# A graph network's second layer: block 11 moves from the count matrices to the gathers

## The chip, the cores and the metric

The kernel runs on one core of a Trainium2 chip. The metric is the device time of one execution in microseconds. Comparisons use the median of several executions; profiles show one execution.

## The reference

6250 nodes with 256 features, 100,000 edges sorted by destination, and a loop at each node. Three graph convolutions, widths 512, 512 and 256, then a residual sum and a layer norm:

```python
deg = jax.ops.segment_sum(jnp.ones_like(dst, dtype=x.dtype), dst, num_segments=n)   # with the loops
dinv = jnp.where(deg > 0, jax.lax.rsqrt(deg), 0.0)
norm_edge = dinv[src] * dinv[dst]
h = x
for W, b in ((W1, b1), (W2, b2), (W3, b3)):
    # h @ W, each edge's source row scaled by norm_edge, summed over its destination, + b
    h = jax.nn.relu(_gcn_layer(h, W, b, src, dst, norm_edge, n))
x = _layernorm(x + h, axis=-1)
```

Since sum and matrix product commute, the kernel sums the scaled rows first and multiplies by W afterwards, where that is cheaper.

## The kernel before

**Blocks and chunks.** The nodes lie in 50 blocks of 125. A block's incoming edges lie in 16 chunks of 128 (`KF`), and what goes beyond them in a chunk that ten blocks share. Each layer sums the neighbours of a block in one of two ways:

- *Gathered*: for each chunk POOL issues an indirect DMA that fetches 128 rows of the layer's table (L1186; in layer 2 a row has 512 floats, 2 KB; in layer 3 it has 256). In layers 2 and 3 ACT casts the landed row to the first part of a two-part number (L1240), DVE takes the rest (L1243), and TensorE multiplies both parts by a one-hot matrix of the destinations, which DVE makes by comparison (L1136), and adds the products in PSUM (L1213: two matmuls of 512 columns for a chunk in layer 2).
- *By count matrices*: in layer 1 the kernel counts, for some blocks, how many edges lead from each node to each node of the block, and keeps these counts as bytes in DRAM (`kept`, 6250 x 125 for a block). A block's sum is then the product of its counts with all 50 blocks of rows.

**Layer 2.** Blocks 0 to 11 are summed by count matrices, in three groups of four (`TEAM`, `TEAMS`), and blocks 12 to 49 are gathered (38 x 16 chunks and a shared one at the first block and at each ten). The generator `teams` does the groups, one after the other. For each of the 50 source blocks (a unit) it loads the rows (two units a load), casts and splits them (L934, L936), casts the counts of the group's blocks from bytes (L926, one cast for each block and five units), and multiplies (L979): four banks, one for each quarter of the 512 features, two matmuls each, with the group's blocks beside each other in the columns, 4 x 125 = 500. After the 50th unit DVE scales each bank by the destinations' `dinv` (L914) and the group's two couples of blocks go through W2 and W3 (`hidden`).

**Order.** There is no scheduler on the chip; the order on each engine is written out by a loop over the chunks in `layer` (L1230). In each step it issues the gather of its chunk, the cast of the chunk three before, the subtraction of the chunk four before, the products of the chunk nine before (six at the end of the layer), and then lets the generators that are due run to their next `yield`, which says after how many chunks they are due again. `teams` yields one chunk for each bank, 23 times in 24 (`PACE`), so that a unit takes about four chunks, whatever its columns are:

```python
if in_layer == 0 and pairs_done % 3 or in_layer == 1 and (pairs_done % PACE if now >= EAGER else pairs_done % 3 == 0):
    yield 1
```

Landed rows of layer 2 go round seven buffers, and their two parts round eight, with three more that are lent as long as the groups run.

**After a block.** `after2` transposes the sum of a gathered block (L1294) and waits for a second one; every two blocks in a row go through W2 and W3 together, and the last two (`ALONE`) alone. `hidden` has one PSUM bank for all (`take("win", 1)`): the products with W2 (L1366, 250 columns for a couple, 125 for one block, eight matmuls in a step), ReLU on ACT (L1372), the products with W3 (L1379), scaling (L1390), and a store to layer 3's table. It waits up to `TO_PE` = 5 chunks between its steps, only one chunk in the last 32 chunks of a layer. The result is also kept in SBUF (`parts`) for layer 3, unless the place is taken by the groups' buffers, which lie over blocks 17 and up (`HOME`); such blocks are read back from the table by `home` once the groups have ended.

**Layer 3** gathers blocks 29 to 49 and sums the others by their count matrices (L1273). Some of its products are made ahead while layer 2's last steps run (L1036). Its first gather waits for the last store of layer 2.

Of the kernel before, what the change touches and what calls it, by code (L numbers as in the profile page):

```python
# [22 lines left out]
P = 128  # L23
# [3 lines left out]
Q = 125  # L27
# [28 lines left out]
EXTRAS_AFTER = (3, 6, 9, 11, 13, 15, 17)  # L56
TEAM = 4
TEAMS = 3
HOME = 17
MANY = 29  # L60
ALONE = 2
# [335 lines left out]
def sorted_path(ctx: ExitStack, tc: tile.TileContext, x, edges, starts, found, wts, biases, room, late, out):  # L397
# [492 lines left out]
    def teams(groups):  # L890

        nonlocal teams_done, returning
        units = [(g, k) for g in range(len(groups)) for k in range(NB)]

        def fetch_counts(g, c):
            for n, b in enumerate(groups[g]):
                by_rows(nc.sync, team_used[(g * CUTS + c) // 2 % 2][n].rearrange("p k v -> p (k v)"), kept[b][:, c * PIECE * Q:(c + 2) * PIECE * Q])

        def next_counts(g, c):
            if c + 2 < CUTS:  # L900
                fetch_counts(g, c + 2)
            elif g + 1 < len(groups):
                fetch_counts(g + 1, c + 2 - CUTS)

        def load(p):
            if 2 * p < len(units):
                k = units[2 * p][1]
                by_rows(nc.sync, streamed[p % RING], tables[1][k * Q:(k + 2) * Q, :].rearrange("(b p) c -> p b c", p=Q))

        def load_scales(g):  # L910
            nc.sync.dma_start(out=scales, in_=dinvs[g * TEAM:(g + 1) * TEAM, :].rearrange("b p -> (b p)").unsqueeze(0).to_broadcast([P, TEAM * Q]))

        def scaled(g, n):
            nc.vector.tensor_tensor(team_zt[:, n], team_banks[n][:, :TEAM * Q], scales, op=ALU.mult)  # L914
            free(f"team{n}")
            if n == TEAM - 1:
                if g + 1 < len(groups):
                    load_scales(g + 1)
                yield SOON
                team_ended[0](hidden(groups[g][:2], team_zt[:, :, :2 * Q], "tz"))  # L920
                for _ in range(4 * KF if g + 1 < len(groups) else 2 * KF):
                    yield 1
                team_ended[0](hidden(groups[g][2:], team_zt[:, :, 2 * Q:], "tz"))

        def piece(g, c, n):
            nc.scalar.copy(team_pieces[(g * CUTS + c) % 2][:, :, n * Q:(n + 1) * Q], team_used[(g * CUTS + c) // 2 % 2][n][:, c % 2 * PIECE:(c % 2 + 1) * PIECE, :])  # L926
            if c % 2 and n == TEAM - 1:
                next_counts(g, c - 1 + 2)

        def half(u, h):  # L930
            if u < len(units):
                to, row = both_parts[u % 3], streamed[u // 2 % RING][:, u % 2, :]
                if h == 0:
                    nc.scalar.copy(to[:, :HID], row)  # L934
                else:
                    nc.vector.tensor_sub(to[:, HID:], row, to[:, :HID].bitcast(F32))  # L936

        while products < FEW * NB - KF:
            yield 1
        fetch_counts(0, 0)  # L940
        for p in range(RING):
            load(p)
        fetch_counts(0, 2)
        yield 6
        load_scales(0)
        while finished < FEW:
            yield 1
        for bank in team_banks:
            while not any(b is bank for b in common):
                yield 1  # L950
            del common[next(n for n, b in enumerate(common) if b is bank)]
        half(0, 0)
        for n in range(TEAM):
            piece(0, 0, n)
            if n % 2:
                yield 1
        half(0, 1)
        half(1, 0)
        yield 1
        half(1, 1)  # L960
        pairs_done = 0
        for u, (g, k) in enumerate(units):
            if u == len(units) - RETURN:
                returning = now
            if u % 2:
                load((u + 1) // 2 + RING - 1)
            for n in range(TEAM):
                if k == 0:
                    yield from take(f"team{n}", 1)
                if k == NB - 1 and n == 0:  # L970
                    while held.get("tz", 0):
                        yield 1
                    held["tz"] = TEAM // 2
                if 1 <= n < 3:
                    half(u + 2, n - 1)
                if k % PIECE == 2 and u + PIECE < len(units):
                    piece(*divmod(g * CUTS + k // PIECE + 1, CUTS), n)
                for h in range(2):
                    nc.tensor.matmul(team_banks[n][:, :TEAM * Q], lhsT=both_parts[u % 3][:, h * HID + n * P:h * HID + (n + 1) * P],  # L979
                                     rhs=team_pieces[(g * CUTS + k // PIECE) % 2][:, k % PIECE, :],  # L980
                                     start=(k == h == 0), stop=(k == NB - 1 and h == 1))
                if k == NB - 1:
                    team_ended[0](scaled(g, n))
                pairs_done += 1
                if in_layer == 0 and pairs_done % 3 or in_layer == 1 and (pairs_done % PACE if now >= EAGER else pairs_done % 3 == 0):
                    yield 1
        teams_done = True
        assert not on_loan, (now, len(on_loan))
# [366 lines left out]
    def hidden(two, zt, name):  # L1355

        wide = len(two) * Q
        each = 4 // len(two)
        yield TO_PE
        yield from take("ht2", 1)  # L1360
        for f2 in range(0, KH, each):
            yield from take("win", 1)
            h_ps = win_bank[:, :4 * Q].rearrange("p (f v) -> p f v", f=each)
            for f in range(each):
                for k in range(KH):
                    nc.tensor.matmul(h_ps[:, f, :], lhsT=w2_sb[:, k, (f2 + f) * P:(f2 + f + 1) * P], rhs=zt[:, k, :],  # L1366
                                     start=(k == 0), stop=(k == KH - 1))
                yield 1
            if f2 + each == KH:
                free(name)  # L1370
            for f in range(each):
                nc.scalar.activation(ht2[:, f2 + f, :wide], h_ps[:, f, :], AF.Relu, bias=b2_sb[:, f2 + f:f2 + f + 1])  # L1372
            yield TO_PE
            free("win")
        yield from take("win", 1)
        u_ps = win_bank[:Q].rearrange("p (h c) -> p h c", h=2)
        for h in range(len(two)):
            for k in range(KH):
                nc.tensor.matmul(u_ps[:, h, :], lhsT=ht2[:, k, h * Q:(h + 1) * Q], rhs=w3_sb[:, k, :],  # L1379
                                 start=(k == 0), stop=(k == KH - 1))  # L1380
            yield 1
        free("ht2")
        u = work.tile([Q, HID], F32, name="st").rearrange("p (h c) -> p h c", h=2)
        if two[-1] == two[0] + 1:
            runs = [(slice(two[0], two[0] + 2), slice(0, 2))]
        else:
            runs = [(slice(p, p + 1), slice(h, h + 1)) for h, p in enumerate(two)]
        for to, h in runs:
            n = to.stop - to.start
            nc.vector.tensor_tensor(u[:, h], u_ps[:, h], dinv[:, to].unsqueeze(2).to_broadcast([Q, n, C]), op=ALU.mult)  # L1390
        for to, h in runs:
            by_rows(nc.sync, u[:, h], tables[2][to.start * Q:to.stop * Q, :].rearrange("(h p) c -> p h c", p=Q), store=True)
            if not teams_done and to.stop > HOME:
                waiting.extend(range(to.start, to.stop))
            else:
                nc.scalar.copy(parts[:, to, :C], u[:, h])
        here = [(to, h) for to, h in runs if to.start not in waiting]
        yield SOON
        for to, h in here:
            nc.vector.tensor_sub(parts[:, to, C:], u[:, h], parts[:, to, :C].bitcast(F32))  # L1400
        yield SOON
        free("win")
# [63 lines left out]
        if b in EXTRAS_AFTER:  # L1466
            made_in_order.append(FEW + EXTRAS_AFTER.index(b))
    assert sorted(made_in_order) == many
    groups = [every[g * TEAM:(g + 1) * TEAM] for g in range(TEAMS)]
    team_steps = teams(groups)  # L1470
    layer(0, C, every[FEW:], few, after1, first_rows, first, spacing, [(0, other_parts()), (2, both_stored(2 * GRP)), (0, searches), (1, counts(made_in_order, places)), (60, dinvs_stored()), (first, team_steps)], carried=team_steps)

# [2 lines left out]
    def last_weights():  # L1475
        load_w2()
        load_w3()
        yield 1
# [3 lines left out]
    split = split_rows_of(two, "swide_split", 1, HID)  # L1482
    split += loaned
    own_row = two.enter_context(tc.tile_pool(name="sown_row", bufs=1)).tile([P, HID], F32, name="own_row")[:Q]
    layer(1, HID, every[TEAM * TEAMS:], [], after2, wide_rows,
          extras=[(5, last_weights()), (0, team_steps), (20, home()), (steps(TEAM * TEAMS) - 2 * KF, fetch_first())], filler=ahead_of_time())
    assert begun % PIECE == 0
    there[:] = [0]
    fetch(many[1], 6)
# [188 lines left out]
```

## Time and profile before

| | |
|---|---|
| three executions | 2067.38, 2073.05, 2081.36 us (median 2073.05) |
| profiled execution | 2076.16 us; its span, from the first to the last instruction, 2074.4 us |
| mean granted TensorE clock | 0.961 |
| busy, share of the span | TensorE 93%, DVE 72%, POOL 68%, ACT 63% |
| DMA | 486.17 MB moved, mean 234 GB/s |

In the profile PE is the matmuls and PEld the weight loads that run under them; L979 is line 979 of the kernel. A row of a group gives engine, operation, tiles (out<-in), count, busy time, the mean of one in ns, and the idle time of the engine just before with what ended most of it. Ends of matmuls are modelled, so a sum of their durations can be more than the time they take; the distance between starts is the better measure. POOL's busy time is that of issuing a gather, not of the transfer.

### The profile page before, as it was taken

Reading aid. Unit: us, or ns where it says so; the run is one execution under the profiler, and the core shown is the slowest. Engines: PE = TensorE matmul, PEld = TensorE weight load, DVE = VectorE, ACT = ScalarE, POOL = GpSimd, SP = SyncE. Lnnn points to the kernel's source line nnn. Section 1 sums busy time; section 2 is a strip of 40 time slices with the busy share of each in tenths; the row PEclk is TensorE's granted clock in tenths of the full one; section 3 lists DMA queues with packets and bytes.
Section 4 is the critical chain, followed back from the end, with each engine's and each line's share of the span. In section 5 each row is a group of like instructions: output and inputs, shape, how many; then the busy total and the mean of one; then the engine's idle time right before and its main releaser. Section 6 shows DMA issues by size and latency. Waiting matters only on the chain. (4 is left out here: it accounts for less than half of the span.)

```text
span 2074.4 us, 30032 instructions
## 1 busy us (share of the span) xinstructions
PE 1923.9 (93%) x8642; PEld 1513.7 (73%) x8642; DVE 1494.1 (72%) x2809; ACT 1302.3 (63%) x2484; POOL 1418.2 (68%) x1442
## 2 busy tenths in 40 slices
PE   4399999999999688999999999999989899999996
PEld 3277777777776467778888878887767777777774
DVE  6877888888882376777766777677675467777776
ACT  2576777787884465766766656667565455556553
POOL 2467777766777377777776776677674577777775
PEclk6699999999999899999999999999999999999998
DMA  7898999999999999999999998978886466666674
GB/s 172 244 308 212 271 260 256 276 260 257 275 274 252 264 268 248 269 260 265 261 262 258 258 260 239 266 230 266 244 239 189 115 180 183 182 178 190 174 191 117
DMA packets 233624, 486.17 MB, mean 234 GB/s; under 512 B 44142, under 2 KB 87358, under 8 KB 233446
## 3 DMA queue, kind: packets, MB, share of 16 engines
q0 software_dynamic: 125184, 315.61, 54.6%
q1 hardware_dynamic: 94980, 159.23, 27.9%
q10 hardware_dynamic: 13282, 9.30, 1.7%
q8 instruction: 70, 1.15, 0.2%
q14 instruction: 108, 0.88, 0.1%
HBM read 416.51 MB, written 67.47 MB: 233 GB/s over the span
## 5 line engine op out<-in xcount | busy, mean ns | idle before, releaser
L1186 POOL DMA_INDIRECT room<-tab,ssrc x1008 | 1025.8, 1018 | 384.6 <-issue 162.6
L1243 DVE TENSOR_TENSOR halves<-room,halves 128x512 fp32r<-128x512 f32 (+1 forms) x806 | 453.4, 579 | 279.0 <-ACT halves L1240 273.0
L1240 ACT CAST halves<-room 128x512 fp32r<-128x512 f32 (+1 forms) x806 | 408.5, 528 | 286.0 <-DMA room<-tab,ssrc 244.7
L1213 PE MATMUL sacc<-halves,shot 128*125 128x512 f32 x1541 | 527.1, 406 | 38.8 <-DVE shot L1136 27.8
L1186 POOL DMA_INDIRECT halves<-both,ssrc x384 | 360.5, 939 | 143.3 <-issue 41.8
L1213 PEld LDWEIGHTS sacc<-halves,shot 128*125 128x125 f32 x1541 | 286.9, 188 | 120.4 <-ACT halves L1240 25.1
L785 DVE TENSOR_TENSOR room<-near_cols,slots 128x625 bf16<-128x625 f32 (+2 forms) x435 | 325.3, 804 | 30.8 <-PE sacc L852 12.7
L1145 ACT CAST piece<-room 125x625 fp32r<-125x625 uint8 x416 | 297.2, 722 | 70.4 <-PE win_ps L1273 19.2
L1136 DVE TENSOR_TENSOR shot<-near_cols,sdlo 128x500 fp32r<-128x500 f32 x371 | 248.0, 670 | 9.3 <-PE sacc L1213 4.8
L1366 PE MATMUL win_ps<-room,w_sb 128*128 128x250 f32 (+1 forms) x832 | 192.5, 375 | 1.6 <-ACT room L1372 1.6
L1273 PE MATMUL win_ps<-parts,piece 125*125 125x512 f32 x650 | 186.2, 405 | 6.2 <-ACT piece L1145 6.2
L1273 PE MATMUL smm<-parts,piece 125*125 125x512 f32 x655 | 188.9, 405 | 1.3 <-ACT piece L1145 0.7
L1366 PEld LDWEIGHTS win_ps<-room,w_sb 128*128 128x128 f32 x832 | 158.0, 195 | 25.3 <-ACT room L1372 2.0
L1273 PE MATMUL mat_ps<-parts,piece 125*125 125x512 f32 x600 | 172.4, 404 | 1.3 <-ACT piece L1145 1.3
L852 PEld LDWEIGHTS <-room 128*125 128x125 bf16 x725 | 95.8, 138 | 74.0 <-issue 23.0
L1273 PE MATMUL sacc<-parts,piece 125*125 125x512 f32 x450 | 147.6, 432 | 0.9 <-ACT piece L1145 0.9
L1273 PEld LDWEIGHTS win_ps<-parts,piece 125*125 125x125 f32 x650 | 119.3, 188 | 37.7 <-ACT piece L1145 8.0
L814 ACT CAST room<-sacc 125x500 uint8<-125x500 f32 (+1 forms) x155 | 107.6, 712 | 56.5 <-PE sacc L852 41.7
L1273 PEld LDWEIGHTS smm<-parts,piece 125*125 125x125 f32 x655 | 116.8, 187 | 29.3 <-issue 2.3
L936 DVE TENSOR_TENSOR parts<-parts 125x512 fp32r<-125x512 f32 x150 | 103.4, 689 | 41.6 <-ACT parts L934 41.6
L1273 PEld LDWEIGHTS mat_ps<-parts,piece 125*125 125x125 f32 x600 | 107.6, 186 | 29.4 <-ACT piece L1145 3.0
L1243 DVE TENSOR_TENSOR parts<-room,parts 128x512 fp32r<-128x512 f32 x138 | 93.4, 692 | 33.3 <-ACT parts L1240 32.9
(310 smaller groups left out, 2938.5 us busy)
## 6 DMA issues: line engine op xcount, KB each, us to landing
parts<-tab SPq DMA_DIRECT2D x81, 448.0 KB
kept<-room SPq DMA_DIRECT2D x29, 683.6 KB
room<-kept SPq DMA_DIRECT2D x29, 683.6 KB
tab<-st SPq DMA_DIRECT2D x74, 224.0 KB
room<-tab,ssrc POOLq DMA_INDIRECT x1008
both<-parts SPq DMA_DIRECT2D x10, 1120.0 KB
own_row<-tab SPq DMA_DIRECT2D x38, 224.0 KB
parts<-kept SPq DMA_DIRECT2D x60, 136.7 KB
```

Of the source, the lines that this page charges most:

```text
L785: nc.vector.tensor_tensor(out, near_cols[:, :shape[2]].unsqueeze(1).to_broadcast(shape), numbers.unsqueeze(2).to_broadcast(shape), op=ALU. ...
L814: nc.scalar.copy(place[:, :, u * G:(u + len(ms)) * G].rearrange("p k (t r) -> p t k r", r=G), counted_in[:Q, :len(ms) * 256].rearrange("p ...
L852: nc.tensor.matmul(bank[:Q, len(pair) * 256:][:, :G * NB], lhsT=hot_lo, rhs=hot_key, start=True, stop=True)
L936: nc.vector.tensor_sub(to[:, HID:], row, to[:, :HID].bitcast(F32))
L1136: nc.vector.tensor_tensor(hot[:, :n], near_cols[:, :Q].unsqueeze(1).to_broadcast([P, n, Q]), dlo.rearrange("p b j -> p (b j)")[:, at:at + ...
L1145: convert(piece, made_or_read[:, c * PIECE:(c + 1) * PIECE, :])
L1186: nc.gpsimd.indirect_dma_start(out=row, out_offset=None, in_=table, in_offset=bass.IndirectOffsetOnAxis(ap=at, axis=0))
L1213: nc.tensor.matmul(acc[:Q, :size], lhsT=hot, rhs=row[:, c0:c0 + size], start=(i == 1 and k == c0 == 0), stop=(k == KF and c0 + size == row ...
L1240: nc.scalar.copy(halves[:, :width], landed[chunk - hi_lag])
L1243: nc.vector.tensor_sub(halves[:, width:], landed.pop(chunk - lo_lag), halves[:, :width].bitcast(F32))
L1273: nc.tensor.matmul(acc_d[:Q], lhsT=got[done // PIECE][:, k % PIECE, :], rhs=parts[:, k], start=(k == 0), stop=(k == NB - 1))
L1366: nc.tensor.matmul(h_ps[:, f, :], lhsT=w2_sb[:, k, (f2 + f) * P:(f2 + f + 1) * P], rhs=zt[:, k, :], start=(k == 0), stop=(k == KH - 1))
```

## The change

The third group has three blocks, 8 to 10, instead of four. Its matmuls read 376 columns instead of 500 (three blocks are 375, made even), the casts and loads of counts of a fourth block are left out, and `hidden` gets block 10 alone as the group's second part. Block 11 is gathered: the layer's list begins with 11 instead of 12, so there are 39 gathered blocks and sixteen chunks more, and the couples are (11,12), (13,14) and so on to (47,48), with 49 alone.

```diff
+IN_TEAMS = 11
...
         def scaled(g, n):
-            nc.vector.tensor_tensor(team_zt[:, n], team_banks[n][:, :TEAM * Q], scales, op=ALU.mult)
+            wide = len(groups[g]) * Q
+            nc.vector.tensor_tensor(team_zt[:, n, :wide], team_banks[n][:, :wide], scales[:, :wide], op=ALU.mult)
...
-                team_ended[0](hidden(groups[g][2:], team_zt[:, :, 2 * Q:], "tz"))
+                team_ended[0](hidden(groups[g][2:], team_zt[:, :, 2 * Q:len(groups[g]) * Q], "tz"))
...
         def piece(g, c, n):
+            if n >= len(groups[g]):
+                return
             nc.scalar.copy(team_pieces[(g * CUTS + c) % 2][:, :, n * Q:(n + 1) * Q], ...)
-            if c % 2 and n == TEAM - 1:
+            if c % 2 and n == len(groups[g]) - 1:
                 next_counts(g, c - 1 + 2)
...
                 for h in range(2):
-                    nc.tensor.matmul(team_banks[n][:, :TEAM * Q], lhsT=both_parts[u % 3][:, h * HID + n * P:h * HID + (n + 1) * P],
-                                     rhs=team_pieces[(g * CUTS + k // PIECE) % 2][:, k % PIECE, :],
+                    nc.tensor.matmul(team_banks[n][:, :-(-len(groups[g]) * Q // 2) * 2], lhsT=both_parts[u % 3][:, h * HID + n * P:h * HID + (n + 1) * P],
+                                     rhs=team_pieces[(g * CUTS + k // PIECE) % 2][:, k % PIECE, :-(-len(groups[g]) * Q // 2) * 2],
                                      start=(k == h == 0), stop=(k == NB - 1 and h == 1))
...
-    groups = [every[g * TEAM:(g + 1) * TEAM] for g in range(TEAMS)]
+    groups = [every[g * TEAM:min((g + 1) * TEAM, IN_TEAMS)] for g in range(TEAMS)]
...
-    layer(1, HID, every[TEAM * TEAMS:], [], after2, wide_rows,
-          extras=[(5, last_weights()), (0, team_steps), (20, home()), (steps(TEAM * TEAMS) - 2 * KF, fetch_first())], filler=ahead_of_time())
+    layer(1, HID, every[IN_TEAMS:], [], after2, wide_rows,
+          extras=[(5, last_weights()), (0, team_steps), (20, home()), (steps(IN_TEAMS) - 2 * KF, fetch_first())], filler=ahead_of_time())
```

## The prediction

> **What bounds the kernel now.** I read the page's first lines, then a table of stretches cut where the trace shows the stages of layer 2 to end, then the groups of instructions in the stretch that the change edits, then single instructions in order of time. The three rounds of count matrices end where the four scalings of their banks stand (921, 1202, 1483 us: first and last start of L914 below). The table's columns are the length of the stretch, then busy time and count of each engine, the granted TensorE clock, the DMA share and GB/s.
>
> ```profile
> span 2074.4 us, 30032 instructions
> PE 1923.9 (93%) x8642; PEld 1513.7 (73%) x8642; DVE 1494.1 (72%) x2809; ACT 1302.3 (63%) x2484; POOL 1418.2 (68%) x1442
> ...
> L914 DVE TENSOR_TENSOR room<-sacc,room x3: 669/669/672, 921.0 to 1483.3; 128x500 f32<-128x500 f32 x3
> ...
> core 0: us, PE busy (x) PEld busy (x) DVE busy (x) ACT busy (x) POOL busy (x), PEclk, DMA share, GB/s
> 750.00:921.00 171.00, 157.87 (x694) 128.62 (x693) 126.20 (x199) 116.38 (x211) 125.06 (x122) 0.98 0.93 260
> 921.00:1202.00 281.00, 274.12 (x1236) 227.40 (x1235) 201.51 (x323) 187.72 (x345) 200.64 (x196) 0.99 0.92 260
> 1202.00:1483.00 281.00, 278.70 (x1249) 232.51 (x1247) 196.98 (x316) 179.12 (x333) 198.50 (x191) 0.99 0.86 248
> 1483.00:1588.00 105.00, 91.23 (x387) 71.92 (x387) 80.04 (x128) 63.90 (x121) 77.03 (x77) 0.95 0.85 242
> 1588.00:1605.00 17.00, 16.46 (x88) 13.44 (x86) 7.18 (x13) 7.39 (x17) 0.94 (x1) 1.00 0.56 157
> 1605.00:1621.00 16.00, 15.54 (x86) 13.17 (x87) 1.77 (x4) 7.43 (x15) 0.29 (x1) 1.00 0.09 25
> 1722.00:2050.00 328.00, 322.52 (x1366) 252.23 (x1366) 243.60 (x654) 188.14 (x444) 251.52 (x252) 1.00 0.67 179
> ```
>
> POOL's count is the number of gathers, so the table gives the time per gathered chunk. It is 171/122 = 1.40 us in the first round's stretch, 281/196 = 1.43 in the second, 281/191 = 1.47 in the third, 105/77 = 1.36 after the rounds, and 328/252 = 1.30 in layer 3. In the third round TensorE is busy for 278.7 of 281 us while DVE, ACT and POOL stand at 64 to 71%: there TensorE sets the pace. In the first round it is 158 of 171 us and DMA is at 0.93 with 260 GB/s: there the transfers are nearly as tight. After the rounds TensorE is at 87%.
>
> Ends of matmuls are modelled, so I test the saturation by starts.
>
> ```profile
> start us, us, engine line op out<-in xcount [idle before <-releaser]
> 1344.74 0.61 PE L979 MATMUL smm<-parts 125*128 125x500 f32 x2
> 1345.19 0.63 PE L1213 MATMUL sacc<-halves,shot 128*125 128x512 f32 x2
> 1345.66 0.62 PE L979 MATMUL str<-parts 125*128 125x500 f32 x2
> ...
> 1585.16 1.86 PE L1366 MATMUL win_ps<-room,w_sb 128*128 128x250 f32 x8
> 1586.67 0.81 PE L1213 MATMUL sacc<-halves,shot 128*125 128x512 f32 x2
> 1587.32 1.85 PE L1366 MATMUL win_ps<-room,w_sb 128*128 128x250 f32 x8
> ...
> 1590.09 1.99 PE L1379 MATMUL win_ps<-w,room 128*125 128x256 f32 x8
> 1591.73 0.82 PE L1213 MATMUL sacc<-halves,shot 128*125 128x512 f32 x2
> 1592.39 1.89 PE L1379 MATMUL win_ps<-w,room 128*125 128x256 f32 x8
> ...
> 1596.87 1.05 PE L1366 MATMUL win_ps<-room,w_sb 128*128 128x125 f32 x8
> 1597.67 0.71 PE L1213 MATMUL sacc<-halves,shot 128*125 128x512 f32 x2
> 1598.22 1.05 PE L1366 MATMUL win_ps<-room,w_sb 128*128 128x125 f32 x8
> ...
> 1603.48 1.28 PE L1213 MATMUL sacc<-halves,shot 128*125 128x512 f32 x4
> ```
>
> Two products of a gathered chunk and two of a round take 1345.66 - 1344.74 = 0.92 us, 0.23 us each, with no room between. With the gathered pair at 0.47, eight of L1366 take 2.16 - 0.47 = 1.69 us at 250 columns and 1.35 - 0.47 = 0.88 at 125, and eight of L1379 take 2.30 - 0.47 = 1.83. So the hidden layer of a couple of blocks costs TensorE 4 x 1.69 + 2 x 1.83 = 10.4 us, that of a single block 4 x 0.88 + 1.83 = 5.4 us.
>
> **What the change removes.** The third round keeps its 50 units x 4 banks x 2 halves = 400 matmuls (L979), but they go from 500 to 376 columns.
>
> ```profile
> L1186 POOL DMA_INDIRECT room<-tab,ssrc x190 | 197.8, 1041 | 81.6 <-issue 38.7 <-DVE halves L1243 27.1 <-DVE parts L1243 6.8
> L1243 DVE TENSOR_TENSOR halves<-room,halves 128x512 fp32r<-128x512 f32 x142 | 95.4, 694 | 54.3 <-ACT halves L1240 53.9 <-PE win_ps L1366 0.3
> L1240 ACT CAST halves<-room 128x512 fp32r<-128x512 f32 x142 | 84.5, 619 | 47.9 <-DMA room<-tab,ssrc 43.5 <-PE sacc L1213 4.3
> ...
> L979 PE MATMUL mat_ps<-parts 125*128 125x500 f32 x100 | 34.1, 422 | 0.0
> L926 ACT CAST parts<-parts 125x625 fp32r<-125x625 uint8 x36 | 25.7, 713 | 0.0
> ```
>
> No row has this kind at 376 columns. From one side it saves nothing, if the time did not go with the columns; from the other all of 0.23 x 124/500 = 0.057 us. The nearest row is L1366, where half the columns saved 0.81 of 1.69 us, 96% of what proportion gives, so I take 0.055 us: 400 x 0.055 = 22 us of TensorE time.
>
> The Trainium skill, TensorE: Matmul & The Clock Gate, section Back-to-back issue gap, gives two rules. The isolated gap is N/2.4 + 2.5 ns, by which 124 columns are worth 52 ns, an estimate of 20.7 us for the 400; the 0.23 us at 500 columns is near that rule's 211 ns. The same section's sustained figures (81 ns at 128 columns, 131 at 512) speak against the change: 16 ns for 124 columns, 6.5 us in all; the 0.23 us in this trace is far above 131 ns. By the first rule the sum below stays as it is, since the transfers bound the gain before TensorE does; by the second the gain is 6.5 instead of 13 us and the time 2083 us, which the fourth rival covers.
>
> Not all of 22 us can come out of the stretch. Its 248 GB/s over 281 us are 69.7 MB; one block's counts fewer (6250 x 125 bytes, 0.8 MB) leaves 68.9. At the 260 GB/s that both earlier stretches reached it needs 265 us, and at the first round's pace of 1.40 us for 191 gathers 267. The next limit is therefore DMA and the seven row buffers behind it, not POOL, whose gathers can start every 1.25 us (rows below; 191 x 1.25 = 239). I take 268: **13 us gained**, bounds 0 (all of it turned into waits) and 22 (TensorE remains the only bound).
>
> The rest that goes is covered: ten of L926's casts (7.1 us of ACT, at 64% in the stretch), a quarter of four scalings on DVE, five fetches of counts. With TensorE's cover gone they would be worth 7 us at most, inside the bound of 22.
>
> **What it adds.** Sixteen gathers of 128 rows of 2 KB, each with a cast (0.62 us), a subtraction (0.69) and two products (0.47), besides four or five comparisons for one-hot rows, a load and a scaling of the block's own row and four transposes. The groups' extra gathers stay at four. The rounds still yield one chunk for each bank and are paced by that count, so they end at the same chunk as now, and what is new comes after them: 94 chunks instead of 78 between the last round and the last gather. There TensorE has slack, and the price of a chunk is its cadence:
>
> ```profile
> 1586.47 0.95 POOL L1186 DMA_INDIRECT room<-tab,ssrc  x1 [0.30 <-issue]
> 1587.99 0.95 POOL L1186 DMA_INDIRECT room<-tab,ssrc  x1 [0.57 <-DVE halves L1243]
> ...
> 1620.70 0.94 POOL L1186 DMA_INDIRECT room<-tab,rest  x1 [31.77 <-issue]
> 1621.95 0.94 POOL L1186 DMA_INDIRECT room<-tab,ssrc  x1 [0.30 <-issue]
> ```
>
> Gathers that wait for nothing start 1621.95 - 1620.70 = 1.25 us apart, the lower bound (20.0 us for sixteen). The stretch after the rounds ran at 1.36, but with the stored blocks being read home at the same time; the first round's 1.40 is the upper bound (22.4). Layer 3's steady 1.30, with lighter rows but no such reads, is nearest: I take 1.31, **21 us lost**.
>
> **What it moves.** The couples of gathered blocks shift by one. Before they are (12,13) to (46,47), and 48 and 49 go alone; after, (11,12) to (45,46), then (47,48), and 49 alone. The round's second couple (10,11) becomes 10 alone. In sum TensorE's hidden work stays the same: 10.4 - 5.4 saved at block 10, the same added at 47/48. Its place does not. Now the last gather starts at 1587.99 and the last product of block 49 ends at 1603.48 + 1.28 = 1604.8, 16.8 us later. In that time TensorE still does the second half of the hidden layer of (46,47) (2 x 1.83 us) and all of 48's (5.4): 9 us of work that was queued behind (44,45) and (10,11) on the one bank for it. With sixteen lighter chunks more after the rounds and half a couple less in the queue, (45,46) is done before the last block begins, and only (47,48) has to fit in: 16 x 0.47 + 10.4 + 0.4 for transposes is 18.3 us of TensorE against 16 x 1.31 = 21 us of gathers. It becomes ready only when 48 has ended, so about half of it falls behind the last gather. I take **5 us gained**, bounds 9 gained (nothing left behind the gather) and 5 lost (all of (47,48) behind it and 49's hidden layer later). After that 49's own hidden layer, its store and layer 3's start follow as now (16 us, filled with products made ahead).
>
> **Sum.** -13 + 21 - 5 = +3 us. The profiled execution took 2076.16 us, so its like would take 2079. It lies 3.1 us over the median of the three runs, 2073.05; the median I expect is 2076. A difference under 1%, 21 us, is about what a measurement of this kernel cannot tell from no change.
>
> **Rivals.**
> - *TensorE is the only bound* of the whole layer: 22 saved, the sixteen chunks at 1.25 us, the tail 9 shorter: -22 + 20 - 9 = -11, 2062 us. For it: 278.7 of 281 us busy, and 92 to 98% in the earlier rounds. Against: DMA share 0.93 in the first round, with a slower chunk than TensorE's work explains.
> - *Slower: the third round does not speed up.* The place is the ring of seven landing buffers: a gather waits until DVE's subtraction has freed its buffer (27.1 + 6.8 us of POOL's idle time above), the cast before it waits for landing (43.5 us on ACT). If these follow DMA's pace, TensorE's 22 us become waits and only the added chunks count: +21, tail unchanged, 2094 us. It decides if the stretch cannot go over some 248 GB/s. Against: 260 GB/s in two stretches.
> - *The tail turns on (47,48).* A couple 5 us dearer than single 48 becomes ready 16 chunks before the end, and 49's hidden layer waits for its bank: -13 + 21 + 5 = +13, 2086 us. Against: the queue ahead of it is shorter than now.
> - *The narrower matmul is no shorter, or hardly*, so that the round is cut in name only: -0 + 21 - 5 = +16, 2089 us. L1366 at two widths speaks against it.
>
> **How the numbers follow.** Forecast 0.48, TensorE alone 0.17, no speed-up 0.19, tail 0.12, no shorter matmul 0.04. The forecast's own range, with 8 to 18 gained in the round and 0 to 8 in the tail, is 2066 to 2086. The range reaches down to TensorE alone (2062) and up to the case without speed-up (2094). Faster by over 1% (under 2052) needs more than all three terms at their best: 0.06. Slower by over 1% (over 2094) is the upper half of the case without speed-up, with some of the tail's on top: 0.14. The rest, 0.80, is within 1%.
>
> **What would show it.** Right: the third round's stretch shrinks to 264 to 271 us with its DMA share at 0.9 or more and TensorE's busy share under 97%; L979's starts 0.17 to 0.18 us apart there; 93 gathers and not 77 between the last scaling and the last gather, 1.28 to 1.36 us apart; the last gather some 8 us later than now, the last product 9 to 14 us behind it instead of 16.8; layer 3 as long as before. Wrong: a stretch at 278 or more (the ring's pace), or at 260 or less with TensorE still full (TensorE alone); a wait of L1366 or L1372 for the bank behind 49's last product (the tail); a change in layer 1 or 3 of more than 5 us, which no step here allows.

## Result, and the profile after

The changed kernel takes 2081.83 us (median of 22 runs) against 2073.59 (22 runs): 8 us more, ratio 1.0040, 95% interval 1.0029 to 1.0052. The profiled execution's span is 2081.1 us against 2074.4.

The table below is the busy time of each engine by stretches, first of the kernel after and then, cut at the same events, of the one before: from the last scaling of the second round to the last scaling of the third, from there to the last gather of layer 2, to its last product, to layer 3's first gather, to the end.

```profile
core 0: us, PE busy (x) PEld busy (x) DVE busy (x) ACT busy (x) POOL busy (x), PEclk, DMA share, GB/s
1207.20:1477.50 270.30, 259.45 (x1245) 225.46 (x1244) 198.87 (x319) 174.28 (x322) 198.17 (x193) 0.98 0.91 257
1477.50:1602.20 124.70, 108.06 (x453) 84.72 (x452) 90.45 (x146) 73.12 (x139) 92.59 (x91) 0.92 0.82 233
1602.20:1615.00 12.80, 12.80 (x57) 9.97 (x55) 5.62 (x9) 6.12 (x13) 0.90 (x1) 1.00 0.67 179
1615.00:1630.30 15.30, 15.24 (x85) 12.73 (x85) 1.60 (x3) 6.97 (x14) 0.00 (x0) 1.00 0.08 24
1630.30:2081.10 450.80, 426.82 (x1790) 333.34 (x1788) 323.16 (x863) 248.82 (x585) 335.16 (x339) 0.97 0.65 173
```

```profile
1204.90:1487.20 282.30, 279.47 (x1257) 232.95 (x1255) 198.12 (x319) 178.22 (x330) 199.73 (x193) 0.99 0.87 249
1487.20:1588.00 100.80, 87.56 (x371) 69.18 (x372) 76.01 (x122) 62.14 (x118) 74.27 (x75) 0.95 0.84 241
1588.00:1604.80 16.80, 16.46 (x88) 13.44 (x86) 7.01 (x12) 7.19 (x17) 0.94 (x1) 1.00 0.57 158
1604.80:1620.70 15.90, 15.24 (x85) 12.91 (x86) 1.94 (x4) 7.63 (x15) 0.00 (x0) 1.00 0.09 25
1620.70:2074.40 453.70, 427.29 (x1789) 332.50 (x1787) 323.33 (x863) 248.44 (x585) 338.16 (x339) 0.97 0.65 172
```

The round gained 12.0 us, the stretch after it lost 23.9, the way from the last gather to layer 3's first gained 4.6 (4.0 of it up to the last product). What stands before (2.3 us later) and layer 3 (2.9 us shorter) do the same work as before, and differences of this size are common between single executions: in the traces of the later runs that leave these parts alone, layer 2 starts between 704.3 and 715.7 us and layer 3 takes 450.2 to 453.2. The sum is 2.3 - 12.0 + 23.9 - 4.6 - 2.9 = 6.7 us, the difference of the spans. The gathers after the round are 91 instead of 75, the sixteen added ones.

In order of time, TensorE in the third round of the kernel after (L983 was L979, L1217 was L1213):

```profile
start us, us, engine line op out<-in xcount [idle before <-releaser]
1341.92 0.51 PE L983 MATMUL mat_ps<-parts 125*128 125x376 f32 x2
1342.27 0.62 PE L1217 MATMUL sacc<-parts,shot 128*125 128x512 f32 x2
1342.73 0.51 PE L983 MATMUL smm<-parts 125*128 125x376 f32 x2
```

Four matmuls take 1342.73 - 1341.92 = 0.81 us instead of 0.92: 0.055 us less for each narrow one, which makes 22 us for 400. TensorE's busy time in the stretch fell by 279.47 - 259.45 = 20 us, but the stretch fell by 12. Where the rest may have gone is seen in the waits of the same stretch, after and then before (engine and line, what it waited for, total us, times, longest):

```profile
ACT halves L1244 <- DMA room<-tab,ssrc: 69.8, 49, 3.6
...
ACT room L1376 <- PE win_ps L1370: 5.2, 3, 3.2
```

```profile
ACT halves L1240 <- DMA room<-tab,ssrc: 43.8, 33, 3.4
...
ACT room L1372 <- PE win_ps L1366: 32.9, 12, 4.5
```

ACT, which had waited 33 us for TensorE inside the hidden layers, now waits 5 us there and 26 us more for gathered rows to land. The later traces have the same pattern: in two more wide rounds (runs 8 and 12 below) the same two lines hold 24 and 23 us for TensorE and 42 and 34 for rows, in three more narrow ones (runs 5, 6 and 9) 9, 4 and 3 us for TensorE and 61, 52 and 69 for rows. TensorE is no longer full (96% of the stretch instead of 99%), and DMA's share rose from 0.87 to 0.91.

### The profile page after: what moved, and what is told of

Read it like the earlier page. It is cut to its first block, busy times and chain, and to the rows that moved or that the text cites. A ratio compares the mean times of both kernels' runs of the same rounds, so it can differ in the third digit from the quotient of the medians.

```text
span 2081.1 us, 30181 instructions
## 1 busy us (share of the span) xinstructions
PE 1918.7 (92%) x8680; PEld 1518.2 (73%) x8680; DVE 1509.9 (73%) x2830; ACT 1307.4 (63%) x2492; POOL 1432.1 (69%) x1458
## 4 chain that ended last, share of the span: by engine, by line
PE 59%; DMA 13%; issue 10%; POOL 6%; DVE 5%; ACT 3%; SPq 0%; ACTq 0%; POOLq 0%; DVEq 0%
PE sacc L1217 12%; DMA room<-tab,ssrc 11%; PE win_ps L1277 6%; POOL room L1190 6%; PE mat_ps L1277 6%; PE smm L1277 5%; PE sacc L1277 5%; PE win_ps L1370 5%; PE win_ps L1383 2%; PE sacc L1324 2%; PE str L1277 2%; PE sacc L983 1%; PE mat_ps L983 1%; PE sacc L853 1%; DVE halves L1247 1%
## 5 line engine op out<-in xcount | busy, mean ns | idle before, releaser
L1190 POOL DMA_INDIRECT room<-tab,ssrc x1024 | 1039.0, 1015 | 383.8 <-issue 168.8
L1247 DVE TENSOR_TENSOR halves<-room,halves 128x512 fp32r<-128x512 f32 (+1 forms) x822 | 465.5, 582 | 285.9 <-ACT halves L1244 280.2
L1244 ACT CAST halves<-room 128x512 fp32r<-128x512 f32 (+1 forms) x822 | 419.4, 530 | 318.9 <-DMA room<-tab,ssrc 274.8
L1217 PE MATMUL sacc<-halves,shot 128*125 128x512 f32 x1575 | 542.9, 411 | 46.1 <-DVE shot L1140 28.5
L1217 PEld LDWEIGHTS sacc<-halves,shot 128*125 128x125 f32 x1575 | 293.5, 190 | 121.4 <-ACT halves L1244 28.4
```

The lines of the kernel that those rows point to most:

```text
L1190: nc.gpsimd.indirect_dma_start(out=row, out_offset=None, in_=table, in_offset=bass.IndirectOffsetOnAxis(ap=at, axis=0))
L1217: nc.tensor.matmul(acc[:Q, :size], lhsT=hot, rhs=row[:, c0:c0 + size], start=(i == 1 and k == c0 == 0), stop=(k == KF and c0 + size == row ...
L1244: nc.scalar.copy(halves[:, :width], landed[chunk - hi_lag])
L1247: nc.vector.tensor_sub(halves[:, width:], landed.pop(chunk - lo_lag), halves[:, :width].bitcast(F32))
```

## Experiments

**The theory** was the prediction's: the narrow round saves TensorE 22 us, of which the transfers let about half through; the sixteen chunks cost their cadence; the tail gains a little. **The rivals:** TensorE as the only bound, waits that no byte count sets, and a price of the moved couples.

Beside the first four kernels the kernel before took 2315.43 us, 12% more than in the other sets of runs (2073.59 to 2077.39). The expectation of run 5 puts this down to another chip; but the first set and the second (runs 5 to 8) carry the same chip number, 6, so that is not shown, and the cause is open.

**1. The narrow round alone.** The changed kernel with block 11 taken out of the gathers again: the third round has three blocks, and block 11 goes through the hidden layer with the columns that the second round left. The sum of block 11 is left out.

```diff
-IN_TEAMS = 11
+IN_TEAMS = 12
...
+        couples, groups = groups, [g[:3] if n == TEAMS - 1 else g for n, g in enumerate(groups)]
...
-                team_ended[0](hidden(groups[g][2:], team_zt[:, :, 2 * Q:len(groups[g]) * Q], "tz"))
+                team_ended[0](hidden(couples[g][2:], team_zt[:, :, 2 * Q:], "tz"))
```

> The kernel before with the third round at 376 columns and three blocks' counts, and block 11 still finished as part of the couple (10,11), from the columns that the second round left there; block 11 is not gathered. Leaves out: the sum of block 11, whose rows are stale. Only the round's width differs from before. Theory (TensorE's saving is cut short by the transfers): the round's stretch falls from 282 to about 270 us and the time by 12 us, to 2062. Rival, TensorE is the only bound: the stretch falls to 260 and the time by 20 to 22, to 2052. Rival, the width costs nothing or the saving is lost in waits: 2072 or more.

Measured: ratio 0.9978 (0.9954 to 1.0003), 5 us less, and by the interval anything from 11 less to 1 more. It can't be told from no change.

**2. The gathers alone.** All rounds as before, and block 11 gathered too, so that it is summed twice and half of one more couple goes through the hidden layer.

```diff
-    layer(1, HID, every[TEAM * TEAMS:], [], after2, wide_rows,
+    layer(1, HID, every[TEAM * TEAMS - 1:], [], after2, wide_rows,
...
```

> The kernel before with all three rounds at four blocks, and block 11 gathered as well (summed twice, with the couples (11,12) to (47,48) and 49 alone). Nothing is left out. Theory (sixteen chunks at the cadence after the rounds, 1.36 us, less a shorter tail, plus one hidden layer more early on): last gather 22 to 24 us later, time +18 to +22, 2091 to 2096. Rival, the chunks are partly hidden in TensorE's slack after the rounds: +12 or less, 2086 or less. Rival, the moved couple (47,48) lengthens the tail: more than 17 us between the last gather and the last product, and +25 or more.

Measured: 1.0083 (1.0058 to 1.0109), 19 us more, as the theory has it.

**3 and 4. Half of the third round's source rows are not loaded**, with the narrow round and with the wide one. The second unit of each load keeps older rows.

```diff
-                by_rows(nc.sync, streamed[p % RING], tables[1][k * Q:(k + 2) * Q, :]...)
+                m = 1 if units[2 * p][0] == TEAMS - 1 else 2
+                by_rows(nc.sync, streamed[p % RING][:, :m], tables[1][k * Q:(k + m) * Q, :]...)
```

> The narrow round of the first run with only one of two source blocks loaded in the third round (25 loads of 250 KB instead of 500 KB; the other half of the buffer keeps older rows). Leaves out: half of the third round's rows and block 11's sum. Theory (transfers are what cut the narrow round's saving short): the rest of the 22 us appears, the stretch falls to 260 to 262 us, time -20, 2053 to 2055. Rival (the rest is lost in waits that bytes do not set, such as the order on ACT): no better than the narrow round alone, 2062.

> The kernel before, wide round, with the same half of the third round's source loads left out (its rows are older ones). Theory (TensorE bounds the wide round): nothing to 4 us gained, 2070 to 2074, TensorE still at 98% or more of the stretch. Rival (the transfers bound the wide round too): 8 us or more gained, 2066 or less.

Measured: 0.9996 (0.9978 to 1.0015) and 1.0001 (0.9982 to 1.0020). Neither did anything that could be told from nothing. For the wide round that is what the theory wants, for the narrow one neither expectation has it. The waits of the whole first kernel suggest why this set is a poor place for the question:

```profile
DVE halves L1248 <- issue: 73.5, 81, 4.6
PEld sacc L1218 <- issue: 61.1, 65, 4.2
```

The engines stand still for 73 and 61 us on "issue" (waits for nothing that the profile shows), up to 4.6 us at a time, where the kernel before in its 2074 us has none and 6 us in the same two lines (L1243 and L1213 there). Small gains in one engine's work may be lost in them. That the engines waited for instructions, as the expectation of run 5 says, goes beyond the profile, which names no cause. All four kernels were run again in sets in which the kernel before takes 2075 and 2077 us.

**5. The narrow round again.**

> The narrow-only kernel once more (third round at 376 columns, block 11 finished from stale columns and not gathered), on another call's chip: the chip of the first four runs is 12% slower with the kernel before (2315 us against 2074) and its engines wait there for instructions. Theory where the kernel before takes some 2074 us: -10 to -14 us. Rival, TensorE is the only bound: -20. Rival, as on the slower chip: -5 or less.

Measured: 2067.74 us against 2075.25, ratio 0.9963 (0.9945 to 0.9982): 8 us less, 4 to 11 by the interval. It misses the range expected by 2 us and rules out the 20 of TensorE alone; a gain of 5 or less, the last rival, is still inside the interval. Its round:

```profile
1213.60:1488.20 274.60, 260.76 (x1256) 226.34 (x1254) 198.10 (x319) 174.33 (x321) 201.76 (x193) 0.99 0.88 254
```

**8. The gathers again.**

> The gather-only kernel once more (all rounds wide, block 11 gathered as well) on this call's chip. Theory: +18 to +22 us where the kernel before takes some 2074 us; with the narrow-only run the two differences add to the change's, within 4 us. Rival (the two parts work on each other): the sum is off by 8 us or more.

Measured: 2087.43 us, ratio 1.0063 (1.0040 to 1.0086): 13 us more (8 to 18), less than expected. With the run before, 13 - 8 = 5 us, against the change's 8: they add, within the 4 us that were asked. Both intervals are some 4 to 5 us wide on either side, so a part of a few us that comes from the two working on each other is not excluded. The stretches of this kernel, as in the first table:

```profile
1204.60:1482.80 278.20, 276.65 (x1256) 231.16 (x1254) 198.74 (x319) 179.89 (x332) 198.34 (x193) 1.00 0.88 252
1482.80:1604.90 122.10, 104.30 (x442) 81.17 (x443) 92.02 (x146) 74.41 (x139) 91.18 (x91) 0.96 0.81 238
1604.90:1619.10 14.20, 14.20 (x63) 11.28 (x61) 5.62 (x9) 6.10 (x13) 0.93 (x1) 1.00 0.60 159
```

The sixteen chunks cost 122.1 - 100.8 = 21.3 us in this trace, 1.33 each, and the tail gains 16.8 - 14.2 = 2.6.

**6. The couples numbered as before.** The changed kernel, with block 11 alone.

```diff
-        if at == 0 and b < NB - ALONE:
+        if at == 0 and b < NB - ALONE and b != IN_TEAMS:
```

> The changed kernel, but block 11 goes through W2 and W3 alone as soon as it is summed, so that the couples are (12,13) to (46,47) and 48 and 49 go alone, as in the kernel before; the sixteen added chunks and the narrow round stay. TensorE has one single block's hidden layer more (5.4 us), early in the layer. Theory (the couples' shift is worth nothing by itself, the tail is shorter because the added chunks come after the queue of hidden layers): within 3 us of the changed kernel, tail from the last gather to the last product 8 to 12 us instead of 12.8. Rival (the shift itself shortened the tail): tail back at 16 to 17 us and 4 us or more slower than the changed kernel.

Measured: ratio to the kernel before 1.0084 (1.0053 to 1.0116), so 9 us slower than the changed kernel. Neither expectation holds as a whole: the tail is shorter, as the theory said, but the stretch after the rounds is longer, and the time with it.

```profile
1208.00:1479.30 271.30, 259.08 (x1244) 225.23 (x1243) 198.02 (x317) 175.70 (x326) 197.17 (x192) 0.98 0.90 256
1479.30:1612.80 133.50, 111.90 (x475) 86.44 (x474) 92.75 (x149) 73.17 (x139) 95.44 (x90) 0.91 0.76 218
1612.80:1621.00 8.20, 7.88 (x38) 5.99 (x36) 4.41 (x9) 3.70 (x9) 0.95 (x1) 1.00 0.79 222
1621.00:1640.00 19.00, 16.74 (x85) 14.13 (x86) 1.60 (x3) 8.34 (x16) 0.00 (x0) 0.91 0.18 54
```

The gathers of the same stretch (90 in the profile against 91) take 133.5 us instead of 124.7, and what the tail gives back (8.2 instead of 12.8 us to the last product) goes again in what follows (19.0 instead of 15.3). TensorE has no more to do there: 111.9 + 7.9 us up to the last product, against 108.1 + 12.8. ACT waits less for rows in the 133.5 us (25.5 against 38.1 us) and more inside hidden layers, for TensorE's products with W2 and for DVE's scaling (22.0 against 8.7).

It matters which couples are moved here. When the second block's sum of (42,43), (44,45) and (46,47) is transposed in the kernel before, 530, 560 and 590 gathers have been issued; for (41,42), (43,44) and (45,46) in the changed kernel 528, 560 and 593; for (42,43), (44,45) and (46,47) in this run 546, 578 and 607. So the changed kernel leaves its hidden layers where they were against the rounds, with one couple more at the end, and it is this run that moves them, by a block's sixteen gathers. The new place and the one hidden layer of a single block that comes on top (5.4 us of TensorE, early in the layer) cost 9 us together; in the two traces the stretches differ after the rounds, where that layer is not. Which wait makes the new place dearer was not tried.

**7. The rounds stretched.** PACE = 1000 in the kernel before.

> The kernel before with PACE = 1000 instead of 24: the rounds' units go one bank a chunk, without the 24th that is done at once, so that the rounds are stretched over some 22 chunks more and end nearer to the last gather. All work stays. Theory (TensorE bounds the rounds and idles after them, so spreading the same work evens it out): the chunk in the rounds falls from 1.47 to 1.44 us and the time by 3 to 10 us. Rival (the queue of hidden layers and the reads home come too late): tail over 20 us and the time up by 5 us or more.

Measured: 1.0043 (1.0024 to 1.0063), 9 us slower. The theory fails, the rival holds for the time but not for its place: the tail is 16.2 us, about as before, and the loss is after the rounds.

```profile
1217.80:1512.90 295.10, 282.96 (x1269) 234.13 (x1268) 207.79 (x330) 188.14 (x342) 218.54 (x202) 0.99 0.86 244
1512.90:1599.90 87.00, 70.27 (x291) 56.21 (x290) 56.72 (x91) 46.37 (x88) 51.81 (x51) 0.90 0.79 222
```

202 chunks in 295.1 us are 1.46 each, no cheaper than 282.3 / 193 = 1.46 before, although TensorE's busy time for a chunk fell from 1.45 to 1.40 us. The bytes for a chunk hardly fell, from 364 to 356 KB by the same rows, which fits a limit by the transfers but does not show it. After the rounds 51 gathers take 87.0 us, 1.71 each.

**11. The rounds pressed together.** PACE = 12.

> The kernel before with PACE = 12 instead of 24: every twelfth bank is done at once, so that the rounds end some 25 chunks earlier. All work stays. Theory (from the run with the pace off, which was 10 us slower because the chunks after the rounds became dearer, 1.70 us): the reverse holds in part, the chunk in the rounds rises to 1.49 to 1.50 us, the chunk after them falls to 1.32 or less and the tail to 12 us or less: -2 to -6 us. Rival (the rounds' dearer chunks take all of it): 0 to +5 us.

Measured: 1.0030 (1.0014 to 1.0047), 6 us slower. The time is near the rival's, but its ground fails as the theory's does, since the chunks in the rounds are no dearer.

```profile
1191.20:1460.30 269.10, 266.06 (x1207) 222.30 (x1206) 191.59 (x308) 174.73 (x323) 188.62 (x184) 1.00 0.89 253
1460.30:1604.30 144.00, 120.32 (x512) 95.18 (x511) 98.35 (x157) 80.23 (x150) 98.82 (x97) 0.93 0.77 215
1604.30:1614.60 10.30, 8.49 (x42) 6.40 (x41) 5.10 (x10) 5.15 (x12) 0.94 (x1) 1.00 0.84 223
```

The round's chunk stays at 269.1 / 184 = 1.46 us and the tail shrinks to 10.3, but the chunks after the rounds cost 144.0 / 97 = 1.48, not 1.32. One stall is large enough to be seen by itself:

```profile
start us, us, engine line op out<-in xcount [idle before <-releaser]
1556.55 1.72 PE L1213 MATMUL sacc<-halves,shot 128*125 128x512 f32 x6
1566.54 1.09 PE L1294 MATMUL sacc<-ident_r,szs 125*128 125x125 f32 x4 [8.28 <-DVE szs L1337]
...
1559.55 0.62 ACT L1240 CAST halves<-room 128x512 fp32r<-128x512 f32 x1 [3.94 <-DMA room<-tab,ssrc]
1562.70 1.14 ACT L1240 CAST halves<-room 128x512 fp32r<-128x512 f32 x2 [2.53 <-DMA room<-tab,ssrc]
```

TensorE stands for 8.3 us before a block's transposes: the scaled sum that they need is queued on DVE behind subtractions, those wait for ACT's casts, and the casts for rows that landed late. POOL was not late: it issued the gathers from 1536 to 1561 us 1.25 to 1.6 us apart, with 0.3 us between two, no more than where nothing holds it. From 1555 to 1564 us the DMA share is at about 1.0; a store, a block's own rows and counts for layer 3 had been issued one after the other at 1551.5 to 1553.3. In the kernel before, the same three go out together (1534 to 1537 us) and TensorE's longest wait after them is 3.4 us. So what made the rows late, and in which order the engines fell into step, stays open.

**9. The dense steps only in the last 16 chunks.** The changed kernel.

```diff
-            most = LATE if chunk < total - 2 * KF else 1
+            most = LATE if chunk < total - KF else 1
```

> The changed kernel, but the steps of a hidden layer are put chunk after chunk only in the last 16 chunks of layer 2 (and of the other layers), not in the last 32. All work stays. Theory (with the steps close together ACT waits for TensorE inside a hidden layer and holds the casts behind it, and so the gathers; the added chunks leave time to spread them): the stretch after the rounds falls from 124 to 117 to 121 us, time 2 to 6 us under the changed kernel. Rival (the queue of hidden layers then runs past the last gather): tail over 15 us instead of 12.8 and 3 us or more slower than the changed kernel.

Measured: 1.0077 (1.0050 to 1.0104) against the kernel before, 8 us more than the changed kernel's 1.0040 by the ratios, with intervals that just meet.

```profile
1211.20:1480.60 269.40, 257.80 (x1254) 225.32 (x1253) 199.44 (x319) 174.02 (x321) 198.43 (x193) 0.99 0.91 258
1480.60:1600.00 119.40, 103.28 (x439) 79.92 (x438) 91.28 (x146) 74.73 (x142) 89.85 (x90) 0.93 0.84 238
1600.00:1617.30 17.30, 15.34 (x61) 12.06 (x59) 5.09 (x9) 4.43 (x10) 0.94 (x1) 0.90 0.53 162
```

Both expectations came true for their places: the stretch after the rounds fell by 5.3 us, to 119.4, and the tail rose by 4.5, to 17.3. In these two traces the density of the steps moves time from the one to the other; there was nothing to win, and the gain in time that the theory expected did not come.

**10 and 12. Half of the source loads again**, narrow and wide.

> Narrow third round with half of its source loads left out, once more, where the kernel before takes some 2074 us (there the narrow round alone gained 8 us, in the stretch 282 or 278 to 270 or 275). Leaves out half of the third round's rows and block 11's sum. Theory (transfers cut the narrow round's saving short): the stretch falls to 258 to 263 us and the time by 17 to 20 us against before. Rival (the rest is lost in waits that bytes do not set): stretch 269 to 275, -8 us as with the narrow round alone.

> The kernel before, wide round, with half of the third round's source loads left out, once more, where the kernel before takes some 2074 us. Theory (TensorE bounds the wide round): the stretch stays at 276 to 282 us, 0 to -4 us. Rival (the transfers bound the wide round as well): 270 us or less, -8 us or more.

Measured: narrow 0.9942 (0.9919 to 0.9965), 12 us less (7 to 17); wide 0.9954 (0.9937 to 0.9972), 10 us less (6 to 13). The third rounds, and for the narrow one the stretch after it:

```profile
1211.70:1475.40 263.70, 256.38 (x1237) 224.69 (x1236) 199.73 (x319) 177.82 (x325) 201.60 (x194) 0.98 0.84 245
1475.40:1580.00 104.60, 91.77 (x386) 72.76 (x385) 75.50 (x122) 61.36 (x117) 77.27 (x75) 0.93 0.82 235
```

```profile
1202.40:1479.30 276.90, 275.31 (x1241) 229.64 (x1240) 199.09 (x319) 181.59 (x333) 201.84 (x194) 0.99 0.81 234
```

| third round | all rows loaded | half of them |
|---|---|---|
| 500 columns | 282.3, 278.2 us (before, run 8) | 276.9 us |
| 376 columns | 270.3, 274.6, 271.3, 269.4 us (after, runs 5, 6, 9) | 263.7 us |

With half of the loads gone the narrow round goes on to 263.7 us, 8 below the mean of the four with all rows and 6 below the least of them. So the stretch of one trace says that the transfers cut its saving short; it is just outside the 258 to 263 of the theory, and the time misses the theory's 17 to 20. ACT's waits for gathered rows say less: with those into the lent buffers they are 66 us, against 67 to 79 in the four. It is not the whole of it: 22 us off the two wide rounds would be 258, and TensorE is still busy for 256 of the 264 us. Of the 8 us, 4 go again in the stretch after the round (104.6 us, against 100.8 in the kernel before), and the time gains 4 us on the narrow round alone, which the intervals do not tell from nothing.

For the wide round trace and times differ. Its stretch hardly moved, as the theory wants, but the time fell by 10 us, as the rival wants, and the one trace starts layer 2 some 5 us earlier than the kernel before, 704.3 against 709.0 us, in work that the edit does not touch. By the times alone, narrowing, halving the loads, and both gain 8, 10 and 12 us, with intervals that overlap. What would fit all of it is that TensorE and the transfers are both close to the limit in these rounds and either's relief is soon stopped by the other. Whether the wide round is held by the transfers as well stays open.

No kernel with all of the work beat the one before.

## Why the prediction was right

- **The round (13 us forecast).** The matmul's price was right, 0.055 us saved for each. The stretch fell to 270 us where 268 was forecast, at 257 GB/s, with DMA at 0.91 and TensorE at 96%, and in one trace half the loads let it fall further. That the transfers are the limit is supported by this, but not proven, since the wide round's time gained from the same halving. By the times of the narrow-only run the gain is 8 us (4 to 11), so the term was some 5 us too large; the 12.0 us of the two profiles holds a slow instance of the round before (282.3, where the gathers' kernel with the same round took 278.2). The rival without any speed-up was right about a part: of TensorE's 22 us, 10 to 14 became waits.
- **The sixteen chunks (21 us).** 23.9 in the changed kernel, 21.3 in the gathers alone. Their place was right: the third round still holds 193 gathers, and all sixteen come after it. The sign named for them failed: the last gather is 14 us later, not 8, since the third round began 2 us later, gained 1 less, and the chunks cost 3 more.
- **The tail (5 us gained).** 4.6 to layer 3's start; the last product 12.8 us behind the last gather, inside the 9 to 14 named. When the last gather was issued, (47,48) had done two of its four steps with W2 and none of its two with W3, so about two thirds of it fell behind, where half was assumed. The rival that it would lengthen the tail fell.
- **The couples.** The prediction priced the moved couples in the tail alone. For this change that was enough: against the rounds the hidden layers stay where they were. The sentence in the expectation of run 6, that the couples' shift is worth nothing by itself, is not borne out: moved against the rounds, and with one small hidden layer more, they cost 9 us.
- **The sum.** +3 forecast, +8 measured; the interval, 6 to 11, leaves +3 out, the stated range holds 2082. By the times, the narrow round gives -8 where -13 was forecast, and the gathers with their tail +13 where +16 was: two misses that make up for each other in part. A sum of +3 from terms that each turned out 3 to 5 us off says little of the sign, and that the kernel became slower, as forecast, is partly luck; what holds is that the two halves nearly cancel. (By its own terms the range starts at 2073 - 18 + 21 - 8 = 2068, not 2066.) TensorE as the only bound would have been 11 us faster than before and is out: 20 us less of its work gave 12 in the profile and 8 by the times.
- **The matmul rules of the Trainium skill** (TensorE: Matmul & The Clock Gate, Back-to-back issue gap). The start-to-start distance at 376 columns is 0.81 - 0.46 = 0.35 us for two, about 0.17 each. The trace agrees with N/2.4 + 2.5 ns (by which 159 ns at 376 columns and 211 at 500 are the estimates) in the slope, 55 ns for 124 columns against its 52, and lies 10 to 20 ns above it; the same section's sustained figures, by which 124 columns are worth 16 ns, do not hold here.

## What to carry to other kernels

When the busiest engine's work is cut in a stretch where another resource stands near its limit too, ask first how far that one lets the stretch shrink: 22 us of TensorE's work were worth 8 us by the times and 12 in the profiles. Work that goes elsewhere is priced by the cadence of the place where it lands, here 1.33 to 1.49 us for a chunk of which TensorE needs a third. And in an order written out by hand the place of work counts as well as its amount: hidden layers moved by sixteen gathers against the rounds, with 5 us of TensorE's work more, cost 9 us here, as much as the whole change.

## What the runs showed of the hardware that I had not expected

The same kernel took 2074 to 2077 us in three sets of runs and 2315 in a fourth, at the same matmul spacing where TensorE does not wait (two products of a chunk and two of a round in 0.92 us). In the profiles of that set the added time is spread as waits over all engines. Their releaser is "issue" (73 us before one line of DVE, 61 before one of TensorE's weight loads) or unnamed (75 us before one line of ACT, called "remote" by the profile, of which the kernel before has none in the profile of its 2074 us). Three edits that gained 8, 10 and 12 us elsewhere gained 5, nothing and 1 us in that set, none of them clear of noise. What causes the waits is not known.
